# 32x32 block transposes on VectorE for the input and the output of a masked attention, with transfers by quadrants of 32 partitions

## The chip, the cores and the metric

The kernel runs on one core of a Trainium2 chip. Five engines work side by side: TensorE (PE in the profile, its weight loads PEld), VectorE (DVE), ScalarE (ACT), GpSimd (POOL) and SyncE (SP, which here only issues transfers). Each takes its instructions in the order of the program and waits for the others through semaphores. Transfers are issued from the queues of SP, POOL and ACT and are carried by 16 DMA engines. The metric is the time of the whole kernel on the device in microseconds (us), as the median of the runs shown. The three runs before the change took 770.23, 771.29 and 773.01 us.

## The reference

The input `x` holds 8 batches of 512 features by 1024 tokens, in float32. The mask `cond_2048` has a 0 or a 1 for each of the 1024 tokens of a batch.

```python
NH = 8; NEG = -1e+30; B, D, T = x.shape; dk = D // NH        # 8, 512, 1024; dk = 64
xt = jnp.transpose(x, (0, 2, 1))
q = xt @ Wq.T
qh = q.reshape(B, T, NH, dk).transpose(0, 2, 1, 3)            # queries, keys and values are the same
scores = scale * jnp.einsum('bhqd,bhkd->bhqk', qh, qh)
cmask = mask[:, None, None, :]
rmask = mask[:, None, :, None]
logits = (scores * cmask + (1.0 - cmask) * NEG) * rmask
attn = jax.nn.softmax(logits, axis=-1)
ctx = jnp.einsum('bhqk,bhkd->bhqd', attn, qh)
ctx = ctx.transpose(0, 2, 1, 3).reshape(B, T, D)
out = ctx @ Wo.T
return x + jnp.transpose(out, (0, 2, 1))
```

A token whose mask is 1 attends to the tokens whose mask is 1. A token whose mask is 0 has logits of 0 everywhere, so its context is the mean of the projected tokens, the same for all of them. About half of the tokens are kept, so a batch needs some 512 real rows and one row for the mean.

## The kernel before

Only kept tokens are computed, in 576 slots (`NK`), cut into five chunks of 128, 128, 128, 128 and 64 (`NC = 5`, `LAST = 4`). The last slot holds the mean token. The rank of each token among the kept ones is worked out in `early`. If a batch kept too many tokens, another function (`attention_of_all_tokens`) would compute everything; it does not run with these inputs.

A batch goes through these steps. `load_batch` brings `x` in as eight tiles of 128 features by 512 tokens. `turn` transposes 128 tokens: TensorE makes four 128x128 transposes into one PSUM bank (L410), ScalarE copies them out (L415), and GpSimd's queue stores them to `xd`, a buffer in HBM with one row per token (L416). `turn` also has ScalarE add up the features for the mean (L425). `search` finds with VectorE which token belongs in each slot (L451), `gather` fetches those rows of `xd` by an indirect DMA (L463), and `collect` turns them back to features by slots, `xc` (L478), and writes the mean into the last slot.

The heads are worked on in pairs, four pairs to a batch and 32 in all. For a pair, `project` computes queries `qT` (L501). `values` turns them to slots by features, `v` (L520), squares `v` with VectorE (L528), and reduces the squares to the largest length (L530, L537). `bias_of` makes of it the shift for the exponentials (L543 to L548). `scores` multiplies a chunk of keys with all queries (L570) and takes the exponentials on ScalarE into `e` (L574). `add_up` sums them with VectorE, two instructions to a chunk (L591). `attend` multiplies `e` with the values (L607), and ScalarE copies the result to `cT` (L623). `inverses` and `invert` make 1/sum and send it through HBM so that it comes back along the free dimension as `rb` (L663 to L685). `contexts` multiplies `cT` by `rb` on VectorE (L695 to L704).

When all four pairs of a batch are done, `output` multiplies the four `cT` with Wo, chunk by chunk (L720), and GpSimd's queue stores the rows to `od` in HBM. `fetch` gathers for each group of 128 tokens its rows of `od` (L791). `finish` transposes four 128x128 blocks on TensorE (L803), adds the input to them on VectorE (L806), and the sum is stored to the output from SP's queue (L808).

The order of all instructions is written by hand. The main loop of `late` goes over pairs p = (b, pr), and in each over the five chunks c. A step of the loop issues, in this order: the scores of chunk c; `add_up` of chunk c-1; at c = 0 the last `add_up` and `invert` of the pair before; `contexts` of the pair before, at c = 2, 3, 3, 4 for pr = 0, 1, 2, 3; at c = 1 `bias_of` the next pair; the work for the next batch; then a share of a list of tasks (`tasks_of`) that TensorE does between scores; then the stores that are due (`issue_stores`). After chunk 4 comes `attend`.

The tasks are the projection and the values of the pair after next, and by pr: for pr = 0 and 1 the turns of batch b+1 (five and three) and `output` of two chunks of batch b-1 each; for pr = 2 `collect` of batch b+1 and the last chunk of `output`; for pr = 3 the eight `finish` of batch b-1. The first `output` of batch b-1 stands in pr = 0 of batch b and needs the `cT` of all four pairs of b-1, the last of which is made by the `contexts` at c = 2 just before it. `search` of batch b+1 is spread over pr = 0, one chunk of slots a step; `gather` stands at the end of pr = 1. In pr = 1 at c = 2 `load_rest` reads `x` of batch b-1 again for the residual; in pr = 2 at c = 0 batch b+2 is loaded. The last batch ends with code of its own (`end_output`, `fetch_last`, `finish_tokens`).

A ring of four PSUM banks (`bank`) serves everything on TensorE but the scores, which have two tiles of two banks. `e` has a ring of six tiles, so VectorE may be most of a pair behind before it holds up a score.

## Time and profile before

| what | value |
|---|---|
| median of three runs | 771.29 us (770.23 to 773.01) |
| the profiled execution | 769.13 us, of which its span 767.4 us |
| mean granted TensorE clock | 0.985 of full speed |
| busy: PE, DVE, ACT, POOL | 721.3, 496.1, 386.8, 200.7 us |
| moved by the 16 DMA engines | 119.52 MB, mean 156 GB/s |
| DMA share by queue: SP (q1), POOL (q0), ACT (q10) | 24.2%, 21.1%, 0.9% |

Times in the profile are in us from the start of the span, if ns is not written. A row for a group of instructions gives the line, the engine, the operation, output and input with their shapes, the number of instructions, their busy time and the mean of one, and then the time that the engine was idle just before them with what ended it. In the chain of waits each piece is the work that held the end at that time. A table by stretches of time gives the busy time of each engine in a stretch, the clock that TensorE was granted (1.00 is full speed), and the share of time in which the DMA engines were busy. PE's instructions overlap, so the length of a run of them in the chain says more than their busy time.

In the middle of the kernel a batch takes about 88.9 us. In the batch from 291 to 380 us its four pairs take 24.6, 23.6, 20.8 and 20.0 us; TensorE is busy for 24.6, 23.6, 20.04 and 19.87 us of them, VectorE for 20.93, 12.32, 12.55 and 15.53 us.

### The profile page before, as it was taken

The page shows a single profiled execution, that of the slowest core. Times are in us where ns is not written, and L with a number is a line of the kernel's source. Part 1 is how long each engine was busy: PE and PEld are TensorE (multiplying, and loading weights), DVE is VectorE, ACT ScalarE, POOL GpSimd, SP SyncE. Part 2 cuts the span into 40 slices and gives each one's busy share as a digit, 9 for nine tenths or more (in the row PEclk, how much of TensorE's full clock was granted, in tenths as well). Part 3 has the DMA queues.
Part 4 walks back from the last instruction along what each step waited for, and adds up shares of the span by engine and source line. Part 5 has one row for each costly group of instructions (what it writes and reads, how often), then busy time and mean ns, then how long its engine had stood idle before and what let it go on. Part 6 is the DMA issues. An engine that isn't in the chain of part 4 may idle for free.

```text
span 767.4 us, 12722 instructions
## 1 busy us (share of the span) xinstructions
PE 721.3 (94%) x4411; PEld 425.1 (55%) x4411; DVE 496.1 (65%) x1495; ACT 386.8 (50%) x783; POOL 200.7 (26%) x264
## 2 busy tenths in 40 slices
PE   6699999999999999999999999999999999899883
PEld 5565565555655556556655556555655566354342
DVE  6287767556975668556984569656785567547453
ACT  3376566644465546545466545645476544245400
POOL 4723003134112413134031432134031340003221
PEclk9899999999999999999999999999999999999996
DMA  7543402556226843447235653357335342146238
GB/s 266 169 166 117 159 18 101 196 165 228 93 108 205 254 166 108 158 144 262 101 141 182 224 195 115 88 207 251 139 128 172 124 135 88 61 155 170 74 128 268
DMA packets 59098, 119.52 MB, mean 156 GB/s; under 512 B 10144, under 2 KB 18400, under 8 KB 59024
## 3 DMA queue, kind: packets, MB, share of 16 engines
q1 hardware_dynamic: 37792, 61.55, 24.2%
q0 software_dynamic: 17008, 54.97, 21.1%
q10 hardware_dynamic: 4224, 2.10, 0.9%
q8 instruction: 37, 0.61, 0.3%
q14 instruction: 37, 0.30, 0.1%
HBM read 75.40 MB, written 43.18 MB: 155 GB/s over the span
## 4 chain that ended last, share of the span: by engine, by line
PE 79%; ACT 5%; DVE 5%; another core or an unknown queue 3%; DMA 3%; issue 2%; POOL 1%; ACTq 0%; POOLq 0%; DVEq 0%
PE s L570 19%; PE av L607 17%; PE pq L501 15%; PE po L720 13%; PE xc L478 4%; PE xt L410 3%; PE o L803 3%; ACT e L574 3%; PE v L520 2%; PE pa L740 2%; DVE junk L591 1%; DMA rank<-ranks 1%; DMA g<-od,origin 1%; ACT v L523 1%
## 5 line engine op out<-in xcount | busy, mean ns | idle before, releaser
L591 DVE CUSTOM_DVE_ANT_0 junk<-e,valid 128x576 f32<-128x576 f32 x256 | 194.9, 761 | 122.4 <-ACT e L574 117.7
L570 PE MATMUL s<-qT 64*128 64x288 f32 (+1 forms) x1280 | 186.3, 434 | 10.6 <-ACT e L574 9.7
L574 ACT ACTIVATE e<-s,bias 128x576 f32<-128x576 f32 x256 | 176.1, 740 | 34.2 <-PE s L570 23.3
L570 PEld LDWEIGHTS s<-qT 64*128 64x128 f32 (+1 forms) x1280 | 93.7, 175 | 97.1 <-issue 58.5
L501 PE MATMUL pq<-xc,wqT 128*128 128x288 f32 x512 | 138.9, 414 | 0.5 <-issue 0.5
L607 PE MATMUL av<-e,v 128*64 128x288 f32 x1024 | 132.6, 409 | 0.8
L720 PE MATMUL po<-woT,cT 128*128 128x512 f32 (+1 forms) x336 | 117.3, 532 | 2.3 <-DVE cT L703 2.3
L501 PEld LDWEIGHTS pq<-xc,wqT 128*128 128x128 f32 x512 | 92.2, 190 | 34.6 <-issue 8.1
L416 POOL DMA_DIRECT2D xd<-xt x64 | 35.5, 558 | 251.3 <-ACT xt L415 250.9
L607 PEld LDWEIGHTS av<-e,v 128*64 128x64 f32 x1024 | 71.0, 137 | 53.5 <-issue 7.2
L623 ACT COPY cT<-av 128x288 f32<-128x288 f32 x62 | 22.3, 401 | 144.5 <-PE av L607 95.3
L720 PEld LDWEIGHTS po<-woT,cT 128*128 128x128 f32 (+1 forms) x336 | 48.2, 173 | 54.7 <-issue 44.1
L729 POOL DMA_DIRECT2D od<-oc x42 | 23.1, 550 | 199.7 <-ACT oc L727 199.7
L791 POOL DMA_INDIRECT g<-od,origin x56 | 59.6, 1065 | 46.0 <-issue 15.7
L508 ACT COPY qT<-pq 128x288 f32<-128x288 f32 x64 | 25.4, 397 | 67.0 <-PE pq L501 64.6
L528 DVE TENSOR_TENSOR sq<-v 128x640 f32<-128x640 f32 x32 | 26.3, 823 | 43.0 <-ACT v L523 36.7
L727 ACT COPY oc<-po 128x512 f32<-128x512 f32 (+1 forms) x35 | 19.2, 550 | 57.0 <-PE po L720 57.0
L463 POOL DMA_INDIRECT xin<-xd,source x40 | 41.6, 1039 | 18.5 <-issue 9.4
L451 DVE TENSOR_SCALAR_CACHE_REDUCE junk<-rank,key 128x1024 f32<-128x1024 f32 (+4 forms) x40 | 40.1, 1002 | 4.1 <-DMA rank<-ranks 2.7
L806 DVE TENSOR_TENSOR xr<-o,xr 128x512 f32<-128x512 f32 x56 | 36.4, 684 | 5.1 <-PE o L803 2.6
L415 ACT COPY xt<-xt 128x512 f32<-128x512 f32 x64 | 35.4, 591 | 2.4 <-PE xt L410 2.1
L425 ACT ACTIVATE junka<-x 128x512 f32<-128x512 f32 x56 | 35.7, 637 | 1.3
(131 smaller groups left out, 698.6 us busy)
## 6 DMA issues: line engine op xcount, KB each, us to landing
xd<-xt POOLq DMA_DIRECT2D x64, 256.0 KB
xr<-in_x_dram SPq DMA_DIRECT2D x64, 256.0 KB
x<-in_x_dram SPq DMA_DIRECT2D x56, 256.0 KB
out_dram<-xr SPq DMA_DIRECT2D x56, 256.0 KB
rb<-row SPq DMA_DIRECT2D x60, 160.0 KB
od<-oc POOLq DMA_DIRECT2D x28, 256.0 KB
rank<-ranks SPq DMA_DIRECT2D x6, 512.0 KB
x<-in_x_dram POOLq DMA_DIRECT2D x8, 256.0 KB
```

Source lines behind the costliest of these rows:

```text
L416: nc.gpsimd.dma_start(xds[b][i * P : (i + 1) * P, :], xt)
L425: nc.scalar.activation(junk, xs[b][d, r], AF.Copy, accum_out=to)
L451: nc.vector.tensor_scalar(junk[:, :n], rank[:, i * P :], key[:, col], 0.0, ALU.is_le, ALU.add, accum_out=found[:, col])
L463: nc.gpsimd.indirect_dma_start(out=xin[:n, :], out_offset=None, in_=xds[b], in_offset=bass.IndirectOffsetOnAxis(ap=searches[b][2][:n, i : ...
L501: nc.tensor.matmul(pq[:, :KH], wqT[:, d, pr * P : (pr + 1) * P], xcs[b][:, d, cols], start=(d == 0), stop=(d == ND - 1),)
L570: nc.tensor.matmul(s[to, h, :KH], qT[heads[h], keys], qT[heads[h], queries], start=True, stop=True)
L574: nc.scalar.activation(e[:, hf if c < LAST else 0, :, :], s[:, :, :KH], AF.Exp, bias=biases[pair][:, c : c + 1], scale=SCALE,)
L591: nc.vector.tensor_tensor_reduce(junk[:, :n].rearrange("p (f k) -> p f k", k=KH), e[:, :, h, :], (valid if c < LAST else part).rearrange(" ...
L607: nc.tensor.matmul(av[head, :KH], v[keys, c, head], e[keys, hf if c < LAST else 0, h, :], start=(c == 0), stop=(c == LAST),)
L720: nc.tensor.matmul(po[k * n : (k + 1) * n, :w], cTs[b, pr][:, i * P : i * P + n], woT[:, pr, k * w : (k + 1) * w], start=(pr == 0), stop=( ...
L791: nc.gpsimd.indirect_dma_start(out=g, out_offset=None, in_=ods[b], in_offset=bass.IndirectOffsetOnAxis(ap=origin[:, b, i : i + 1], axis=0),)
L806: nc.vector.tensor_tensor(xr, pt, xr, ALU.add)
```

## The change

Five things are changed together.

1. For batches 1 to 7 the input is turned by VectorE. `x` is loaded with four neighbouring features in a partition, as two tiles of 128 x 4 x 512. A `turn` is now one VectorE instruction that transposes 32x32 blocks over 256 tokens (128 x 1024 elements), so there are four turns to a batch in place of eight. The turned tile is stored to `xd` by four transfers, one for each quadrant of 32 partitions, from SP's queue, in runs of 512 bytes. The turns stand at (pr, c) = (0, 0), (0, 2), (0, 4) and (1, 1). Batch 0 is turned on TensorE as before (`turn_first`).
2. ScalarE still adds up the features, now as eight steps of their own over pr = 0 and 1. Because of the new order of features the sums go through HBM and back by two small transfers (`mean_of`).
3. For batches 0 to 5 (`BLOCKS`) the output is turned by VectorE too. `fetch` uses other indices (`block_origin`), so that a 32x32 block transpose of the fetched rows gives features by tokens. `finish_blocks` transposes 128 x 512 elements on VectorE and adds the input on VectorE. The eight of a batch stand at c = 2, 3 and 4 of pr = 3 (two each) and at c = 0 and c = 1 of pr = 0 of the next batch. `load_rest` and the store of the output use four transfers a batch, each of 32 partitions, in runs of 1024 bytes; before there were eight each, of 128 partitions in runs of 2048 bytes.
4. `search` moves from pr = 0 to pr = 1.
5. The squares in `values` are taken by ScalarE.

Batch 6 is still finished on TensorE, at the end, and batch 7 by its own code.

```diff
+    def turn_first(i):
+        r, at = divmod(i * P, NB)
+        pt = bank(f"xt_0_{i}")
+        for d in range(ND):
+            nc.tensor.transpose(pt[:, d * P : (d + 1) * P], xs[0][r][:, d, at : at + P], ident)
...
     def turn(b, i):
-        r, at = divmod(i * P, NB)
-        pt = bank(f"xt_{b}_{i}")
-        for d in range(ND):
-            nc.tensor.transpose(pt[:, d * P : (d + 1) * P], xs[b][d, r][:, at : at + P], ident)
...
-        nc.scalar.copy(xt, pt)
-        nc.gpsimd.dma_start(xds[b][i * P : (i + 1) * P, :], xt)
-        if i % G == G - 1 and b:
-            means(b, r)
+        n = T // NQ
+        r, at = divmod(i * n, NB)
...
+        nc.vector.transpose(
+            xt.rearrange("p k (f d) -> p k d f", d=ND),
+            xs[b][r][:, :, at : at + n].rearrange("p d (k t) -> p k d t", t=Q),
+        )
+        def store():
+            for a in range(A):
+                to = xds[b][i * n : (i + 1) * n, a * P : (a + 1) * P]
+                nc.sync.dma_start(
+                    to.rearrange("(k t) c -> t k c", t=Q), xt[a * Q : (a + 1) * Q, :, :]
+                )
+        stores[1].append(store)
...
+    def mean_of(b):
+        total = sb.tile([P, ND], F32, tag="total", name=f"total_{b}")
+        nc.vector.tensor_tensor(total, xbars[b][:, :, 0], xbars[b][:, :, 1], ALU.add)
...
+        nc.sync.dma_start(row, total)
+            nc.sync.dma_start(xmeans[b], row.rearrange("(a f) d -> (f d) a", a=A))
...
-        nc.vector.tensor_tensor(sq, v, v, ALU.mult)
+        nc.scalar.activation(sq, v, AF.Square)
...
     def load_rest(b):
+        xr = sb.tile([P, D // Q, T // A], F32, tag="xr", name=f"xr_{b}", bufs=1)
+        if b in BLOCKS:
+            for a in range(A):
+                nc.sync.dma_start(xr[a * Q : (a + 1) * Q, :, :], in_blocks(x[b])[a])
...
+    def finish_blocks(b, i):
+        o = sb.tile([P, D // Q, Q], F32, tag="o", name=f"o_{b}_{i}", bufs=2)
+        nc.vector.transpose(o.rearrange("p k t -> p (k t)"), gs[b, i])
+        xr = xrs[b]
+        to = xr[:, :, i * Q : (i + 1) * Q]
+        nc.vector.tensor_tensor(to, o, to, ALU.add)
+        if i == NT - 1:
+            def store():
+                for a in range(A):
+                    nc.sync.dma_start(in_blocks(out[b])[a], xr[a * Q : (a + 1) * Q, :, :])
+            stores[0].append(store)
...
+        TURN = [(0, 0), (0, 2), (0, 4), (1, 1)]
+        FINISH = {
+            (ND - 1, 2): (0, 1),
+            (ND - 1, 3): (2, 3),
+            (ND - 1, 4): (4, 5),
+            (0, 0): (6,),
+            (0, 1): (7,),
+        }
...
                 if b + 1 < B:
-                    if pr == 0:
+                    if (pr, c) in TURN:
+                        turn(b + 1, TURN.index((pr, c)))
+                    if pr < 2 and pr * NC + c < NN * ND:
+                        add_features(b + 1, pr * NC + c)
+                    if pr == 1 and c == LAST:
+                        mean_of(b + 1)
+                    if pr == 1:
                         search(b + 1, c)
...
+                if p == 2 and c == 2:
+                    place_blocks()
+                for i in FINISH.get((pr, c), ()):
+                    of = b - 1 if pr == ND - 1 else b - 2
+                    if of in BLOCKS and of >= 0:
+                        finish_blocks(of, i)
```

## The prediction

> **What bounds the kernel now.** I read the page's totals and its chain first.
>
> ```profile
> PE 721.3 (94%) x4411; PEld 425.1 (55%) x4411; DVE 496.1 (65%) x1495; ACT 386.8 (50%) x783; POOL 200.7 (26%) x264
> PE 79%; ACT 5%; DVE 5%; another core or an unknown queue 3%; DMA 3%; issue 2%; POOL 1%; ACTq 0%; POOLq 0%; DVEq 0%
> PE s L570 19%; PE av L607 17%; PE pq L501 15%; PE po L720 13%; PE xc L478 4%; PE xt L410 3%; PE o L803 3%; ACT e L574 3%; PE v L520 2%; PE pa L740 2%; DVE junk L591 1%; DMA rank<-ranks 1%; DMA g<-od,origin 1%; ACT v L523 1%
> ```
>
> TensorE carries the end, and the transposes that go, xt and o, are on the chain. By that alone the change would pay. VectorE, at 65%, gets the work, but a share of 65% is an average, so I asked for the groups by shape, for the chain through one batch, and for the timeline where pr = 3 meets the next pr = 0.
>
> ```profile
> L410 PE MATMUL xt<-ident,x 128*128 128x128 f32 x256 | 36.0, 287 | 0.0
> L803 PE MATMUL o<-ident,g 128*128 128x128 f32 x224 | 30.9, 278 | 0.0
> L806 DVE TENSOR_TENSOR xr<-o,xr 128x512 f32<-128x512 f32 x56 | 36.4, 684 | 5.1 <-PE o L803 2.6 <-issue 2.5
> L528 DVE TENSOR_TENSOR sq<-v 128x640 f32<-128x640 f32 x32 | 26.3, 823 | 43.0 <-ACT v L523 36.7 <-ACT el L574 3.2 <-issue 3.1
> L677 DVE STREAM_TRANSPOSE rt<-ris 128x32 f32<-128x32 f32 x30 | 6.3, 212 | 1.0
> L950 DVE COPY spread<-totals 64x256 f32<-64x256 f32 x1 | 0.3, 285 | 0.0
> ```
>
> To see: the mean of a TensorE transpose is not its price, since they overlap; the only VectorE transpose here is 32 elements long.
>
> The chain through the batch from 291 to 380 us gives prices:
>
> ```profile
> 299.22 1.17 PE s L570 x8
> 300.39 1.02 PE xt L410 x8
> ...
> 316.91 1.46 PE xt L410 x12
> ...
> 364.79 1.31 PE o L803 x12
> ```
>
> And the place that decides, in the timelines of an ordinary batch and of batch 7:
>
> ```profile
> 363.61 0.76 DVE L591 CUSTOM_DVE_ANT_0 junk<-e,valid 128x576 f32<-128x576 f32 x1 [3.57 <-ACT e L574]
> 389.76 3.70 PE L720 MATMUL po<-woT,cT 128*128 128x512 f32 x8
> 390.65 0.76 DVE L703 TENSOR_TENSOR cT<-cT,rb 128x576 f32<-128x576 f32 x1
> ```
>
> ```profile
> 653.08 2.84 PE L720 MATMUL po<-woT,cT 128*128 128x512 f32 x6
> 657.44 0.76 DVE L703 TENSOR_TENSOR cT<-cT,rb 128x576 f32<-128x576 f32 x1
> 658.26 1.41 PE L720 MATMUL po<-woT,cT 128*128 128x512 f32 x2 [2.33 <-DVE cT L703]
> ```
>
> `output` needs the fourth `cT` for its last two matmuls of eight. In the ordinary batch they are due at 389.8 + 6 x 0.456 = 392.5 (the chain has 3.65 us for eight) and `cT` is ready at 391.4: about 1 us of slack, and VectorE has worked almost without a pause since 363.61. Batch 7 has no turns behind it; there TensorE came early and stood for 2.33 us. So in pr = 3 and the start of the next pr = 0 VectorE is already nearly the bound.
>
> ```profile
> 656.00:658.00 2.00, 0.00 (x0) 0.00 (x0) 1.86 (x7) 0.00 (x0) 0.00 (x0) 1.00 0.00 0
> 658.00:660.00 2.00, 1.74 (x4) 0.71 (x6) 1.79 (x6) 0.30 (x1) 0.00 (x0) 0.74 0.00 0
> 660.00:662.00 2.00, 2.00 (x9) 0.96 (x8) 0.00 (x0) 1.09 (x3) 0.59 (x1) 0.50 0.14 59
> 662.00:664.00 2.00, 2.00 (x5) 0.98 (x6) 1.26 (x3) 0.67 (x1) 0.00 (x0) 0.90 0.19 76
> ```
>
> After that wait the granted clock (third column from the end) fell to 0.50. From 658.26 to the next `attend` at 666.42 took 8.16 us; the same pieces in an ordinary batch take 0.9 + 1.17 + 3.63 + 0.65 = 6.35. The clock cost 1.8 us.
>
> **The change part by part.**
>
> *Off TensorE.* A batch loses 4.1 us in pr = 3 (pieces of 12, 4, 8, 4 and 4 transposes: 1.31 + 0.59 + 1.02 + 0.59 + 0.59), 2.3 in pr = 0 (0.87 + 0.44 + 1.02) and 1.46 in pr = 1. Over 6 finished and 7 turned batches that is 6 x 4.1 + 7 x 3.8 = 51 us. This is the most that can be won.
>
> *Price of a VectorE transpose.* No row shows a long one. Low end: L950, 285 ns for 256 elements against 153 ns for a one-element copy (L704), 0.52 ns an element, so 0.42 us for 512 and 0.69 for 1024. High end: L677, 212 ns for 32 against 153 for one, 1.9 ns an element, so 1.13 and 2.1. I take one element a cycle, as every two-input row (0.68 for 512, 0.82 for 640): 0.71 and 1.24, because L677 stands only 20 ns above what those rows give for 32. Back to back each hides some 0.08 us of its tail behind the next, unless that one needs its result.
>
> *VectorE from the first `add_up` of pr = 3 (363.61) to `cT` in the next pr = 0 (391.41): 27.8 us.* Off: eight adds, 8 x 0.62 = 5.0; one square, 0.85; `search` 0 and 1, 1.40 + 1.24; short waits for TensorE and `rb` that a later VectorE no longer has, 1.3. On: eight `finish_blocks`, transpose 0.74 with its gap, then add 0.62, 10.9; turn 0, 1.16; length and top of the values, 0.93, which stood behind `contexts` and now stand ahead (TensorE reaches `values` at c = 1). Sum: +3.2 us, so `cT` at 394.6. TensorE is there 6.4 us earlier, at 386.1, and waits 8.5 us. It resumes 394.6 - 392.5 = 2.1 us later than before, and loses 1.8 us by the clock: **+3.9 us**, five times (batches 1 to 5 into the next) = +19.5. Into batch 7 there is no turn, and the wait and the lost clock were there before: 628.03 + 29.2 = 657.2 against 658.2, -0.9.
>
> *pr = 1.* Six times -1.46 = -8.8. VectorE takes five searches (5.9) and turn 3, less a square: 12.3 + 5.9 + 1.2 - 0.8 = 18.6 of 22 us. The last `source` comes about 2 us before the pair's end, while the fifth gather was issued 1.3 us after it until now. If that cover is gone `collect` is late: +1 to 2 a batch.
>
> *Batch 0.* The chain stands on ranks for 7.6 us until 42.1 and then on VectorE to 60. With searches gone from pr = 0 TensorE needs 17.8 of the 21.6 us: -3.8. The next pair loses 1.46 and gets five searches (VectorE 18.8, TensorE 14.9); I give back 1.8. Sum -3.5. In batch 1's pr = 0, 2.3 us of turns go, and a wait of some 1.6 us and perhaps the clock come: 0, between -2.3 and +1.
>
> *Early part.* Eight sums of 512 (5.4 us, on the chain) become two of 2048, by the slope 2.3 each: -0.9. `place_blocks`, 16 copies of some 0.15 in batch 0's third pair, where VectorE is idle 8 us of 21: nothing; uncovered 2.4.
>
> *ScalarE.* 56 copies of 0.59 go (33), 32 squares of some 0.75 come (L425's 0.64 for 512), 24. The squares stand before the copies of `cT`, under `attend`'s 4.7 us, or beside scores: nothing; each could delay an exponential by 0.75.
>
> *Queues.* POOL loses 56 issues of 0.55 that nobody waited for. SP gains 112 stores of some 0.35 and 14 transfers of the mean, and loses 48. It waits for a turn, but its next urgent item, the rows of `invert`, comes only in the next pair; behind turn 3 stands only `load_rest`. The mean's two hops, like `invert` to `rb`, take about 8 us, and there are some 11 till `project` needs them. The 512-byte runs to HBM cost nothing extra: ACT's queue moved 4224 packets of about 500 bytes for 0.9% of the 16 engines, 26 ns each, no dearer by the byte than SP's 79 ns for 1629. Quadrants: no row shows a long transfer of 32 partitions. From nothing up to `rb` 3 us late; I take nothing, since the turned rows are issued behind `rb`.
>
> *Sum:* 19.5 - 0.9 - 8.8 - 3.5 - 0.9 = **+5.4 us**. The profiled execution took 769.1 us, span 767.4, so 774.5 there; the median was 771.3, 2.2 above it, so **776.7**.
>
> The Trainium skill, "TensorE: Matmul & The Clock Gate", "Why this matters for your kernels", asks for no idle gaps over about 3 us. The trace is harsher, as 2.33 us sufficed. By the page's window of 3.4 us at half speed a wait would cost 1.7 us in place of 1.8, and the sum would be 0.5 lower. "SBUF — State Buffer", "Door 1: The DMA port swizzle", speaks against the change: 32 partitions reach 8 of 16 ports, 189 GB/s. By it a reload of 2 MB is an estimated 11 us, against about 5.5 at the 380 to 400 GB/s seen here with 128; the sum gets no term, because pr = 1 has room for it.
>
> **The rivals.**
>
> *The relief comes whole* (faster): 771.3 - 51 = 720. For it: the chain's 79%. Against: `cT` would have to come 8.5 us earlier.
>
> *Cheap transposes* (faster): at the low end the stretch is 8 x 0.29 + 0.55 = 2.9 shorter, 5 x 2.9 + 2.3 = 17 less: 760. For it: L950. Against: L677.
>
> *The clock holds*: 5 x 1.8 less, 768. For it: at 712 to 716 TensorE was idle for 2.2 us and the clock stayed 1.00. Against: at 16 to 24 and at 746 to 750 longer gaps halved it.
>
> *Dear transposes* (slower): at the high end 8 x 0.42 + 0.86 = 4.2 longer, 5 x 4.2 + 3.4 = 24 more: 801.
>
> *Transfers late* (slower): `rb` came 7.8 us after its transpose, and four of five such `contexts` waited 0.27 to 0.69 us for it. It has some 0.5 us to spare now. With 3 us of delay, five times 2.5: 789.
>
> **How the numbers follow.** About 0.3% (2.3 us) can be told from no change. Forecast 0.45 (own range 768 to 786), cheap transposes 0.12, clock holds 0.10, whole relief 0.04, dear transposes 0.15, late transfers 0.14. Slower: 0.32 + 0.15 + 0.13 = 0.60. Same: 0.07 of the forecast and 0.06 of the clock and the transfers. Faster: the remaining 0.27. Range 757 to 801, from the two ends of the transpose.
>
> **What would show it.** A 512-element STREAM_TRANSPOSE near 0.71 us; "PE po <- DVE cT L703" near 8 us in each of six batches, with clock 0.50 after it; VectorE without idle time from pr = 3 to that `cT`; pr = 1 about 1.4 us shorter. I am wrong if TensorE does not wait there, if `collect` or `rb` waits for a DMA, or if exponentials come late behind squares.

## The result and the profile after

The change made the kernel slower: 817.8 us (median, 814.8 to 823.5) against 770.8 for the kernel before beside it, a ratio of 1.0625 (95% interval 1.0551 to 1.0699). I had forecast 776.7. The direction was right and the size was not. The profiled execution took 823.5 us, with a span of 821.7.

First the totals and the chain of the kernel after, by engine and by line.

```profile
PE 707.9 (86%) x3995; PEld 393.8 (48%) x3995; DVE 556.7 (68%) x1550; ACT 381.7 (46%) x759; POOL 165.6 (20%) x208
...
PE 52%; DVE 25%; DMA 9%; issue 7%; ACT 4%; POOL 1%; SPq 0%; another core or an unknown queue 0%; POOLq 0%; DVEq 0%; ACTq 0%
PE s L614 12%; PE po L764 12%; PE av L651 11%; PE pq L545 9%; DMA xin<-xd,source 6%; DVE junk L635 6%; DVE o L841 3%; DVE xr L844 3%; ACT e L618 3%; DVE xt L446 2%; PE xc L524 2%; DVE junk L497 2%; DVE cT L747 2%; PE pa L784 1%; DVE len L574 1%
```

TensorE's share of the chain fell from 79% to 52%. VectorE took 25% in place of 5%. And there is a newcomer that my sum didn't hold: the gather of tokens, `xin`, with 6%. TensorE's busy time fell by only 13 us although 416 instructions are gone, because much of the rest ran at a lower clock (mean 0.927 in place of 0.985).

The groups by shape give the prices that were unknown:

```profile
L446 DVE STREAM_TRANSPOSE xt<-x 128x1024 f32<-128x1024 f32 x28 | 57.6, 2059 | 0.4 <-DMA rank<-ranks 0.4
L841 DVE STREAM_TRANSPOSE o<-g 128x512 f32<-128x512 f32 x48 | 33.8, 704 | 0.0
L844 DVE TENSOR_TENSOR xr<-o,xr 128x512 f32<-128x512 f32 x48 | 33.2, 693 | 1.6
L574 DVE TENSOR_REDUCE len<-sq 128x10 f32<-128x640 f32 x32 | 26.0, 813 | 33.3 <-ACT sq L572 22.6 <-issue 8.4 <-ACT v L567 2.3
```

The transpose of 512 elements took 0.70 us, as forecast. The one of 1024 took 2.06, where I had put 1.24. The last line shows something I had costed at nothing: VectorE stood 22.6 us for ScalarE's squares.

The waits (in total, times, longest) and the places where they stand in TensorE's timeline (the number in brackets is the idle time before the instruction):

```profile
PE po L764 <- DVE cT L747: 48.3, 7, 8.4
PE xc L524 <- DMA xin<-xd,source: 31.1, 8, 9.4
```

```profile
362.89 1.09 PE L524 MATMUL xc<-ident,xin 128*128 128x128 f32 x4 [4.29 <-DMA xin<-xd,source]
...
408.09 2.84 PE L764 MATMUL po<-woT,cT 128*128 128x512 f32 x6
418.87 2.08 PE L764 MATMUL po<-woT,cT 128*128 128x512 f32 x2 [7.94 <-DVE cT L747]
```

The stall for the fourth `cT` is the one I forecast: 7.8 to 8.4 us in batches 2 to 6, 5.3 in batch 7, 2.8 in batch 1. VectorE worked without a pause between these two rows, from the first `add_up` of pr = 3 to that `cT`:

```profile
387.23 0.76 DVE L635 CUSTOM_DVE_ANT_0 junk<-e,valid 128x576 f32<-128x576 f32 x1 [3.54 <-ACT e L618]
...
418.06 0.76 DVE L747 TENSOR_TENSOR cT<-cT,rb 128x576 f32<-128x576 f32 x1
```

The stall for `xin` is the one I missed: at the start of pr = 2, `collect` waits 3.4 to 4.3 us for the gathered tokens, in six batches. (The 31.1 us also hold the 9.4 us at the kernel's start, which were there before.)

To see what each costs I took the starts of `attend` from TensorE's timeline. The table has the time from the `attend` of the pair before to that of the pair named, medians over batches 2 to 6, worked out from those starts.

| us | pr = 0 | pr = 1 | pr = 2 | pr = 3 | batch |
|---|---|---|---|---|---|
| before | 24.5 | 23.6 | 20.7 | 20.1 | 88.9 |
| after | 33.4 | 22.6 | 26.1 | 16.0 | 98.1 |
| forecast | +8.0 | -1.5 | 0 | -4.1 | +2.4 |
| measured | +8.9 | -1.0 | +5.4 | -4.1 | +9.2 |

The forecast for pr = 3 and pr = 0 together was +3.9, of which -4.1 lay in pr = 3; +4.8 was measured. So one column is far off, pr = 2: 5.4 us a batch where the sum had none. What it waits for is in the timelines of SP and POOL and in the windows (busy time of PE, PEld, DVE, ACT and POOL, granted clock, share of the DMA engines, GB/s) of the same batch:

```profile
345.83 1.86 SPq L454 DMA_DIRECT2D xd<-xt  x4
347.73 2.14 SPq L829 DMA_DIRECT2D xr<-in_x_dram  x4
...
353.43 1.03 POOL L509 DMA_INDIRECT xin<-xd,source  x1 [0.56 <-DVE cT L748]
```

```profile
348.00:350.00 2.00, 2.00 (x6) 0.80 (x6) 1.93 (x6) 0.72 (x2) 0.00 (x0) 1.00 0.88 215
350.00:352.00 2.00, 2.00 (x13) 0.56 (x11) 1.86 (x8) 0.55 (x1) 0.00 (x0) 1.00 0.99 221
...
354.00:356.00 2.00, 2.00 (x20) 1.20 (x18) 1.93 (x9) 0.28 (x1) 1.51 (x2) 1.00 1.12 205
356.00:358.00 2.00, 2.00 (x22) 0.93 (x20) 1.93 (x7) 0.31 (x1) 1.58 (x2) 1.00 1.12 189
358.00:360.00 2.00, 0.61 (x6) 0.15 (x2) 1.62 (x11) 0.49 (x2) 1.27 (x2) 1.00 1.10 223
360.00:362.00 2.00, 0.00 (x0) 0.00 (x0) 0.00 (x1) 1.37 (x2) 0.00 (x0) 0.64 1.05 390
362.00:364.00 2.00, 1.10 (x6) 0.81 (x8) 1.53 (x4) 0.00 (x0) 0.00 (x0) 0.50 0.75 263
```

SP issues in order. The reload of x stands behind the four stores of turn 3, turn 3 comes late from a full VectorE, and so the reload starts at 347.7, 13.0 us after pr = 1's first scores (334.8). In the kernel before it started 2.8 us after them (at 318.5; the scores at 315.7). The DMA engines then look full (share 0.88 to 0.99 before the gather, 1.05 to 1.12 with it) and move only 189 to 223 GB/s until 360. The gather is issued at 353.4 into the middle of that. In the kernel before the reload ran in windows like these, and the first gather was issued at 335.1, when it was long over:

```profile
318.47 5.79 SPq L771 DMA_DIRECT2D xr<-in_x_dram  x8
335.12 1.04 POOL L463 DMA_INDIRECT xin<-xd,source  x1 [0.38 <-issue]
...
322.00:324.00 2.00, 2.00 (x6) 0.95 (x5) 0.69 (x4) 1.73 (x5) 0.00 (x0) 1.00 1.02 380
324.00:326.00 2.00, 2.00 (x11) 0.88 (x9) 1.30 (x4) 0.68 (x2) 0.00 (x0) 1.00 1.01 390
```

### The profile page after: what moved, and what is told of

Same layout as the page of the kernel before. It is cut to its first block, busy times and chain, and to the rows that moved or that the text cites. A ratio compares the mean times of both kernels' runs of the same rounds, so it can differ in the third digit from the quotient of the medians.

```text
span 821.7 us, 11761 instructions
## 1 busy us (share of the span) xinstructions
PE 707.9 (86%) x3995; PEld 393.8 (48%) x3995; DVE 556.7 (68%) x1550; ACT 381.7 (46%) x759; POOL 165.6 (20%) x208
## 4 chain that ended last, share of the span: by engine, by line
PE 52%; DVE 25%; DMA 9%; issue 7%; ACT 4%; POOL 1%; SPq 0%; another core or an unknown queue 0%; POOLq 0%; DVEq 0%; ACTq 0%
PE s L614 12%; PE po L764 12%; PE av L651 11%; PE pq L545 9%; DMA xin<-xd,source 6%; DVE junk L635 6%; DVE o L841 3%; DVE xr L844 3%; ACT e L618 3%; DVE xt L446 2%; PE xc L524 2%; DVE junk L497 2%; DVE cT L747 2%; PE pa L784 1%; DVE len L574 1%
## 5 line engine op out<-in xcount | busy, mean ns | idle before, releaser
L614 PE MATMUL s<-qT 64*128 64x288 f32 (+1 forms) x1280 | 193.7, 447 | 6.7 <-ACT e L618 4.7
L764 PE MATMUL po<-woT,cT 128*128 128x512 f32 (+1 forms) x336 | 139.3, 637 | 48.3 <-DVE cT L747 48.3
L614 PEld LDWEIGHTS s<-qT 64*128 64x128 f32 (+1 forms) x1280 | 96.9, 182 | 103.5 <-issue 61.9
L764 PEld LDWEIGHTS po<-woT,cT 128*128 128x128 f32 (+1 forms) x336 | 54.9, 208 | 113.7 <-issue 58.0
L446 DVE STREAM_TRANSPOSE xt<-x 128x1024 f32<-128x1024 f32 x28 | 57.6, 2059 | 0.4 <-DMA rank<-ranks 0.4
L870 POOL DMA_INDIRECT g<-od,block_origin x48 | 50.2, 1046 | 34.6 <-issue 30.3
L589 DVE TENSOR_REDUCE m<-top 128x1 f32<-128x128 f32 x32 | 9.3, 290 | 68.8 <-PE top L587 68.8
L524 PE MATMUL xc<-ident,xin 128*128 128x128 f32 (+1 forms) x160 | 24.5, 296 | 34.5 <-DMA xin<-xd,source 31.1
L574 DVE TENSOR_REDUCE len<-sq 128x10 f32<-128x640 f32 x32 | 26.0, 813 | 33.3 <-ACT sq L572 22.6
L635 DVE CUSTOM_DVE_ANT_0 junk<-el,part 128x288 f32<-128x288 f32 x64 | 29.1, 454 | 15.2 <-ACT el L618 13.9
```

The source lines that it names most:

```text
L446: nc.vector.transpose(xt.rearrange("p k (f d) -> p k d f", d=ND), xs[b][r][:, :, at : at + n].rearrange("p d (k t) -> p k d t", t=Q),)
L524: nc.tensor.transpose(pt[:, d * n : (d + 1) * n], xin[:n, d * P : (d + 1) * P], ident[:n, :n])
L574: nc.vector.tensor_reduce(lengths, sq.rearrange("p c (h d) -> p (c h) d", h=2), axis=AX.X, op=ALU.add,)
L614: nc.tensor.matmul(s[to, h, :KH], qT[heads[h], keys], qT[heads[h], queries], start=True, stop=True)
L635: nc.vector.tensor_tensor_reduce(junk[:, :n].rearrange("p (f k) -> p f k", k=KH), e[:, :, h, :], (valid if c < LAST else part).rearrange(" ...
L764: nc.tensor.matmul(po[k * n : (k + 1) * n, :w], cTs[b, pr][:, i * P : i * P + n], woT[:, pr, k * w : (k + 1) * w], start=(pr == 0), stop=( ...
```

## The experiments

The kernel before did not take the same time in all comparisons: about 759 us in some, 770 to 776 in others (the last experiment looks at this). Ratios are always to the kernel before beside it. Times are compared directly only where the kernel before took 758.7 to 759.2 us beside both; there the changed kernel took 815.1 us, ratio 1.0733 (1.0705 to 1.0762).

> The changed kernel itself, so that the other three runs stand beside it on one chip: ratio 1.055 to 1.07.

It came out a little above, since the kernel before was faster there. The stalls were the same: 7.8 to 8.0 us for `cT` in batches 2 to 6, 3.5 to 4.3 for `xin`.

### The reload: its place and its width

Place alone:

```diff
-                if pr == 1 and c == 2 and b > 0:
+                if pr == 1 and c == 0 and b > 0:
                     load_rest(b - 1)
```

> The changed kernel with one edit: load_rest(b - 1) is called at (pr 1, c 0) in place of (pr 1, c 2), so that its four transfers stand ahead of turn 3's stores on SP's queue. In the profile after, TensorE stands 3.4 to 4.3 us at the first xc of pr = 2 in six batches (sum 23.1 us), and the clock is granted at 0.50 to 0.66 for some 6 us after it. Theory 'queue place': SP waits for turn 3, issues the reload 12.9 us after the pair's start, and the gather shares the DMA engines with it. Then here the reload is issued within 4 us of the pair's start, is over before the gather at about +18.6 us, the wait for xin is under 1 us each, and the time falls by 23 to 35 us, to about 786. Rival 'the gather is late by itself' (the last source comes from a full VectorE at +18.4 us): the waits stay at 3 to 4 us and the time stays within 4 us of 818.

Width and length of runs:

```diff
-            for a in range(A):
-                nc.sync.dma_start(xr[a * Q : (a + 1) * Q, :, :], in_blocks(x[b])[a])
+            wide = xr.rearrange("p k n -> p (k n)")
+            for i in range(NN * ND):
+                r, d = divmod(i, ND)
+                nc.sync.dma_start(
+                    wide[:, i * NB : (i + 1) * NB],
+                    x[b, d * P : (d + 1) * P, r * NB : (r + 1) * NB],
+                )
```

> The changed kernel with the reload at its late place, but as eight transfers of 128 partitions with runs of 2 KB, as the kernel before had it, in place of four of 32 partitions with runs of 1 KB. The features of x then stand at other places of xr than the rows that are added to them, so that the output isn't the reference's; the work and the bytes are the same. Theory 'rate': the reload ran at 190 to 220 GB/s from 348 to 360 us in the profile after, while the kernel before moved the same bytes at 380 to 400. Here it takes 5 to 6 us from +12.9, ends at about +18.5 as the gather begins, the wait for xin falls below 1.5 us each and the time falls by 15 to 35 us. If only the place on the queue matters, part of the overlap stays and the waits stay above 2 us; if the gather is late by itself, nothing changes.

Width alone, with runs of 1 KB in four transfers as in the change:

```diff
-            for a in range(A):
-                nc.sync.dma_start(xr[a * Q : (a + 1) * Q, :, :], in_blocks(x[b])[a])
+            wide = xr.rearrange("p (j k) n -> j p k n", j=A)
+            parts = x[b].rearrange("(k p) (j n) -> j p k n", p=P, j=A)
+            for j in range(A):
+                nc.sync.dma_start(wide[j], parts[j])
```

> The changed kernel with the reload at its late place, in four transfers of 512 KB with runs of 1 KB, as in the change, but each over 128 partitions in place of 32. The features of x then stand at other places of xr than the rows added to them, so that the output isn't the reference's; bytes, runs and places on the queue are the same. Theory 'partitions': the reload takes 5 to 7 us in place of some 12 and the waits for xin fall below 2.5 us, as in the kernel with wide transfers and runs of 2 KB (784 us where the changed kernel took 815). Rival 'length of the runs': it takes 10 us or more, the waits stay at 3.4 to 4.3 us, and the time stays within 6 us of the changed kernel's.

| | us | ratio | pr = 2 |
|---|---|---|---|
| the change | 815.1 | 1.0733 (1.0705 to 1.0762) | 25.9 |
| reload ahead of turn 3 | 786.7 | 1.0354 (1.0323 to 1.0385) | 20.2 |
| reload in 128 partitions, 2 KB | 784.2 | 1.0342 (1.0324 to 1.0360) | 20.5 |
| reload in 128 partitions, 1 KB | 782.0 | 1.0292 (1.0260 to 1.0325) | 20.2 |

Each of the three brings pr = 2 back to its old length, so it takes both causes to make the stall: a reload that is late and one that is slow. Each is worth 28 to 33 us. This is the largest part of the loss that I missed. In the first of the three the reload was issued 2.2 us after pr = 1's first scores. The last run separates what the second had changed together: the same bytes in the same runs of 1 KB, but over 128 partitions, moved in these windows:

```profile
340.00:342.00 2.00, 2.00 (x15) 0.73 (x13) 1.86 (x7) 1.08 (x2) 0.29 (x1) 1.00 1.08 355
342.00:344.00 2.00, 2.00 (x18) 1.20 (x18) 1.93 (x6) 1.63 (x4) 1.28 (x2) 1.00 1.10 360
344.00:346.00 2.00, 2.00 (x18) 1.00 (x14) 1.93 (x8) 0.00 (x0) 1.55 (x2) 1.00 1.07 382
```

355 to 382 GB/s against 189 to 223 at the same share of the engines: the partitions make the difference, not the runs. The fast windows end at 346, some 9 us after the reload was issued (337.1) behind turn 3's stores, so the 5 to 7 us are not shown; the waits for `xin` behind the start of the kernel came to 2.8 us in all. The Trainium skill, "SBUF — State Buffer", "Door 1: The DMA port swizzle", gives 189 GB/s for 32 partitions at 1 MiB and about 218 as the limit; the two windows before the gather, 215 and 221, agree. The prediction had an estimate of 11 us from that page, and I then gave it no term.

The wait for `cT` did not move with any of this, here in the run with the reload ahead:

```profile
PE po L764 <- DVE cT L747: 47.6, 7, 8.1
PE xc L524 <- DMA xin<-xd,source: 15.5, 7, 9.7
```

### The price of the turn

```diff
         nc.vector.transpose(
-            xt.rearrange("p k (f d) -> p k d f", d=ND),
+            xt.rearrange("p k (d f) -> p k d f", d=ND),
```

> The changed kernel with the turn's output written block behind block (32 elements in a row) in place of with a stride of 4 elements. The features of a row of xd then stand in another order, so that the output isn't the reference's; count and size of all instructions and transfers are the same. Theory 'stride of the output': the instruction of 1024 elements falls from 2.06 to between 1.25 and 1.40 us (twice the 0.70 us of the 512-element one, which is written densely). It stands once on VectorE's chain to cT (0.7 us, five or six times, 4 us) and once on that to the gather (0.7 us, six times, 4 us): 6 to 9 us less in all. Rival 'stride of the blocks that are read' (a new row of d every 32 elements) or 'two ports, other cause': it stays at 2.06 us and the time stays the same.

```profile
L446 DVE STREAM_TRANSPOSE xt<-x 128x1024 f32<-128x1024 f32 x28 | 34.8, 1241 | 0.4 <-issue 0.4
```

Written densely, 1024 elements took 1.241 us, which is the price I had taken. The stride of four elements in what it writes makes it 2.06. The waits for `cT` fell from 7.8 to 7.1 us, and the time was 803.1 us, ratio 1.0584 (1.0542 to 1.0625), 12 us below the changed kernel: a little more than the 6 to 9 expected. By the starts of `attend`, pr = 0 became 5.8 us shorter in all and pr = 2 4.7, so that part of these 12 us lies within the stall for `xin`.

### One part of the change alone

The input part, with outputs turned on TensorE as before:

```diff
-    BLOCKS = range(B - 2)
+    BLOCKS = range(0)
...
+            elif b + 1 < B:
+                t = 0.5
+                back += [(t, lambda r=r, d=d: finish(b - 1, r, d)) for r in range(NN) for d in range(ND)]
```

> The changed kernel with BLOCKS = range(0) and the eight finish tasks of 0.5 back in pr = 3: tokens turned on VectorE, outputs turned on TensorE as before, reload in 128 partitions. Theory 'two stalls make the loss' (the wait for cT at 7.8 to 8.4 us in five batches from finishes and turn 0 on VectorE; the wait for xin from the quadrant reload): here VectorE loses 8 x 0.64 us ahead of cT, so the wait for cT is 0 to 3 us, the wait for xin 0 to 1.5 us, and what TensorE loses in transposes (7 x 3.8 us) is a gain in part: 750 to 768, centre 757. Rival 'turn 0 and the searches in pr = 1 are what cost, whatever becomes of the output': 775 or above, waits for cT above 4 us or for xin above 3 us.

766.0 us, ratio 1.0100 (1.0082 to 1.0118): inside the band in us, but the gain that the text counted on did not come, since the kernel before took 758.7 beside it. The wait for `cT` is 2.8 us in six batches and 2.2 in the seventh (18.9 in all) and the clock is at 0.50 for some 3.4 us after it, which eats what TensorE no longer does.

The output part alone, in the kernel before (`finish_blocks`, its reload, its places as in the change):

> The kernel before with the output part alone: eight finish_blocks of VectorE for each of batches 0 to 5 in place of TensorE's transposes, with the reload by quadrants at its old place (to fit the memory, xt has 4 buffers and pa lies in those of xin). Theory of the two stalls: VectorE gets 8 x (0.64 + 0.69) less 8 x 0.62 and some waits, 4.4 us, ahead of the fourth cT; TensorE comes 4.1 us earlier against 1 us of slack: it waits 7 to 7.5 us in five or six batches, resumes 3.3 us later than in the kernel before and loses some 1.8 us of clock, so +5 us each: ratio 1.03 to 1.045. The reload starts 3 us into pr = 1 with no turns ahead of it, so no wait for xin over 1 us. Rival 'the output part is harmless by itself and only meets turn 0 badly': ratio 0.97 to 1.00, waits for cT under 4 us.

Ratio 1.0264 (1.0186 to 1.0341), a little below the expected band, though its interval reaches into it, and not in the form expected. TensorE's waits in that run:

```profile
PE po L722 <- DVE cT L705: 17.8, 6, 7.0
PE s L572 <- ACT e L576: 15.6, 32, 1.5
PE v L522 <- DVE m L547: 9.6, 5, 1.9
...
PE top L545 <- DVE top L539: 6.6, 6, 1.2
```

The wait came in pieces: 1.2 us for `top`, 1.9 for `m` and 1.5 to 3.2 for `cT` in each of the five batches, 6.95 only in the last. All three are results of VectorE, in pr = 0, which took 31.1 us in place of 24.5.

The squares alone:

```diff
-        nc.vector.tensor_tensor(sq, v, v, ALU.mult)
+        nc.scalar.activation(sq, v, AF.Square)
```

> The kernel before with the squares alone moved: sq by ScalarE's Square in place of VectorE's product. My prediction put this part at nothing. Theory 'hidden': ratio to the kernel before 0.995 to 1.003. Rival 'a new wait': in the input-only kernel VectorE stood 1.95 us for ScalarE's square directly ahead of add_up and contexts (len L574 <- ACT sq), and in the profile after 22.6 us in six such waits; if that happens here too, up to eight times 2 to 4 us, and where it delays cT, 1.005 to 1.03.

Ratio 0.9991 (0.9952 to 1.0029): nothing, as predicted. The three parts add up to 0.0100 + 0.0264 - 0.0009 = 0.0355, and the change with its reload ahead has 0.0354. That they agree so well proves little: the kernel before took 776.2 us beside the last two parts and 758.7 beside the others. What the waits do show is that the stall for `xin` comes only when the parts meet. With the input part alone these waits make 6.0 us in all behind the start of the kernel, with the output part alone there are none. The late turn 3 of the one pushes the slow reload of the other into the gather.

### Is it the order of the work, or a full VectorE?

The stall for `cT` has two sides: VectorE is late, and TensorE asks early. First I let TensorE ask later, with the outputs of the batch before a whole pair later:

```diff
-                mine = {0: (0, 1), 1: (2, 3), 2: (4,)}[pr]
+                mine = {0: (), 1: (0, 1, 2), 2: (3, 4)}[pr]
```

> The whole change with the reload ahead of turn 3's stores (ratio 1.0354), and the output tasks moved a pair later as in the run beside it. There TensorE waited 7.8 to 8.1 us for the fourth cT in five batches, 2.8 and 5.3 in two others (47.6 us), with about 3.5 to 6 us of half clock after each. Theory 'order, not load': VectorE's late cT is needed 7.2 us of work later, the five waits fall below 1.5 us each, 45 to 60 us less, ratio 0.955 to 0.98: the change then pays. Rival 'VectorE is the bound in pr = 3 to pr = 0': add_up and contexts stay late, the wait comes back at bias, at the exponentials or at the first output of pr = 1, ratio 1.00 to 1.035.

> The input-only kernel (ratio 1.0100) with one edit: the output tasks of batch b - 1 stand at pr = 1 (0, 1, 2) and pr = 2 (3, 4) of batch b in place of pr = 0 (0, 1), 1 (2, 3) and 2 (4), so that 7.2 us of TensorE's work that needs the fourth cT stands a pair later. In the input-only run TensorE waited 2.8 us for that cT in six batches and 2.2 in the seventh (18.9 us) with the clock at 0.50 for some 3.5 us after it (1.7 us each). Theory 'TensorE's work was put in an order that needs cT too early': these waits go, 25 to 31 us less, ratio 0.96 to 0.98, and the transposes taken off TensorE (27 us) come through. Rival 'VectorE or ScalarE bounds pr = 0 anyway': other waits of the same sum take their place (for e, for rb, for project's copies), ratio 0.99 to 1.01.

With the whole change the rival was right, and more than that: ratio 1.0607 (1.0536 to 1.0678), worse than 1.0354 (in us 825.1 against 786.7). The wait for `cT` is gone, and pr = 0 takes 16.1 us in place of 32.7. But pr = 1 now takes 26.9 and pr = 2 35.7. The chain of that run shows where the time went:

```profile
332.47 2.07 DVE xt L446
...
338.46 1.21 SPq L454
339.71 1.26 SPq L454
341.01 10.58 DMA xd<-xt
...
352.38 3.31 DMA xin<-xd,source
355.82 1.09 PE xc L524 x4
```

VectorE worked from 288 to 338 with hardly a pause (9.4 to 9.7 us of each 10). TensorE ran ahead of it through the pair, and what came late then was turn 3; its stores needed 10.6 us beside the reload, and TensorE waited 9.3 to 10.0 us for `xin` in five batches. A stall that is moved without its cause comes back where the next result of the full engine is needed.

With the input part alone, ratio 0.9935 (0.9901 to 0.9970). The waits for `cT` went, and waits for `e` of 3.0 to 4.5 us appeared at pr = 3 in five batches. There ScalarE itself stood for something that the trace doesn't name (2.48 us at 453.7), as it did in the kernel before (the last experiment). That is what the rival had said, in number and in kind. Spreading the same input part further (turns at (0, 2), (0, 3), (0, 4), (1, 0), and one output a pair later) brought nothing measurable:

> The input-only kernel (ratio 1.0100, waits for cT of 2.8 us) with turn 0 behind the contexts of pr = 0, turns at (0, 2), (0, 3), (0, 4), (1, 0), and one output a pair later. Theory 'place': the waits for cT go (18.9 us and some 12 us of clock) and those for xin too; ratio 0.965 to 0.985. With no output in pr = 0 at all (ratio 0.9935) waits for e of 3 to 4.5 us took their place at pr = 3; if these are there here too, 0.985 to 0.995.

Ratio 0.9992 (0.9953 to 1.0030), with the same waits for `e`, above both bands that I had given. Both runs stood beside a kernel before of 772 to 776 us and had stalls of that unnamed kind themselves, so what the order of the input part is worth without them stays open.

Then I took the work away from the place where VectorE is full: the finishes run a batch later, where VectorE has room.

```diff
         FINISH = {
-            (ND - 1, 2): (0, 1),
-            (ND - 1, 3): (2, 3),
-            (ND - 1, 4): (4, 5),
-            (0, 0): (6,),
-            (0, 1): (7,),
+            (2, 0): (0,), (2, 1): (1,), (2, 2): (2,), (2, 3): (3,), (2, 4): (4,),
+            (3, 0): (5,), (3, 1): (6,), (3, 2): (7,),
         }
...
-                if pr == 1 and c == 2 and b > 0:
-                    load_rest(b - 1)
-                if pr == 3 and c == 0 and b > 0:
+                if pr == 1 and c == 0 and b > 1:
+                    load_rest(b - 2)
+                if pr == 3 and c == LAST and b == B - 1:
+                    load_rest(b - 1)
+                if pr == 3 and c == 3 and b > 0:
                     fetch(b - 1)
...
-                    of = b - 1 if pr == ND - 1 else b - 2
+                    of = b - 2
```

> The whole change with its eight finish_blocks a batch later: five in pr = 2 (one a step) and three at the start of pr = 3, the gather of the outputs at (pr 3, c 3), the reload at (pr 1, c 0) of that batch, ahead of turn 3's stores. Nothing is left out; VectorE does the same work. With the finishes at their first place and the reload ahead, the ratio was 1.0354 and TensorE waited 7.8 to 8.1 us for the fourth cT in five batches. Theory 'place on VectorE': 10.7 us leave the stretch from pr = 3's first add_up to that cT, the wait falls to the 2.8 us of the input-only kernel, and what TensorE no longer turns (51 us) comes through in part: ratio 0.955 to 0.985. Rival 'VectorE is too full anywhere' (with the outputs a pair later, the 7.9 us came back as a wait for xin of 9 to 10 us): pr = 2 now has the late add_up, waits for e or cT of pr = 1 of the same sum appear there, ratio 1.01 to 1.04.

Ratio 0.9801 (0.9734 to 0.9868) where the kernel before took 772.2 us. Where it took 759.1, the same kernel gave 756.8 us and 0.9967 (0.9945 to 0.9990), outside what I had expected, because the kernel before was faster there; the waits came as said:

> The kernel with the finishes a batch later, once more: ratio 0.973 to 0.987, waits for the fourth cT of 2.2 to 3.1 us in seven batches.

```profile
PE po L764 <- DVE cT L747: 19.0, 7, 2.8
```

VectorE does as much work as in the change, and the time is 58 us less than the changed kernel's 815.1. Against the run with only the reload ahead (786.7) it is 30 us, and pr = 0 shows them: 26.8 us in place of 32.7. (In the profiles pr = 0 is 38 us shorter in all seven batches together, and the end of the kernel is 8 us longer, where TensorE now waits up to 7.4 us for gathered outputs.) So place is what cost, not the amount of work. A wait of 2.8 us for `cT` stayed. The prediction's own step would put it on turn 0, so I moved turn 0 behind it, first together with one output, then alone:

```diff
-        TURN = [(0, 0), (0, 2), (0, 4), (1, 1)]
+        TURN = [(0, 2), (0, 3), (0, 4), (1, 0)]
```

> As the run beside it, and with turn 0 behind the contexts of pr = 0 (turns at (0, 2), (0, 3), (0, 4), (1, 0)) and one output of batch b - 1 a pair later (1, 2 and 2 in pr = 0, 1 and 2). Theory 'place': turn 0's 2.1 us leave the way to cT too, and the output that needs it comes 3.6 us later: waits for cT under 1 us, turn 3 earlier by some 6 us, no wait for xin, ratio 0.945 to 0.965. Rival 'VectorE too full': no better than the run beside it, or above 1.00.

> The finishes a batch later, and the turns alone at (0, 2), (0, 3), (0, 4), (1, 0), so that turn 0 comes behind the fourth cT. By the prediction's step (turn 0 stands on the way to cT: 1.16 us, 2.06 as measured) it gains 7 x 2 = 14 us at most, ratio 0.96 to 0.975. Rival: the turns are bunched, VectorE and SP fall behind in pr = 1 and the gather comes late, as in the run with the output moved too (waits for xin of 3.2 to 6.5 us, ratio 1.0112): 1.00 to 1.015.

Neither gained. The first was slower, 1.0112 (1.0047 to 1.0177): pr = 0 shrank to 21.8 us, but pr = 2 grew to 29.9, with waits for `xin` of 3.2 to 6.5. With the turns alone pr = 2 is 20.4, so that was the moved output. The turns alone: 763.1 us, 1.0050 (1.0028 to 1.0073), 6 us slower than beside it, and the wait for `cT` still 2.8 to 3.1 in six batches. The rows of ScalarE, VectorE and TensorE there show what it hangs on:

```profile
381.22 0.75 ACT L568 COPY v<-v 128x512 f32<-128x512 f32 x2
...
382.00 0.74 ACT L573 ACTIVATE sq<-v 128x640 f32<-128x640 f32 x1
...
382.77 0.82 DVE L575 TENSOR_REDUCE len<-sq 128x10 f32<-128x640 f32 x1 [1.95 <-ACT sq L573]
...
386.51 0.76 DVE L748 TENSOR_TENSOR cT<-cT,rb 128x576 f32<-128x576 f32 x1
...
387.32 2.08 PE L765 MATMUL po<-woT,cT 128*128 128x512 f32 x2 [2.80 <-DVE cT L748]
```

VectorE is not full here. It stands 1.95 us for ScalarE's square, because the length of the values is ahead of `contexts` in its order, and the values themselves have just come from TensorE; from there to `cT` it works without a pause. With no transposes to do in pr = 0, TensorE reaches `values` and then the outputs sooner than this round can close. That is read from one batch's rows: no run gave the squares back to VectorE in this kernel. So at last I let TensorE ask one step later, not a whole pair:

```diff
                 mine = {0: (0, 1), 1: (2, 3), 2: (4,)}[pr]
+                if pr == 0:
+                    end.append((6.0, lambda: None))
```

> The kernel with the finishes a batch later (ratio 0.9801), and in pr = 0 an empty task of weight 6.0 ahead of the two outputs of batch b - 1, so that they come at c = 3 and 4 in place of 2 and 3, behind one more step of scores. There TensorE still waited 2.8 to 3.1 us for the fourth cT in six batches and 2.2 in the seventh (19.2 us), and lost about 1.7 us of clock after each: rb is issued at 381 to 382 us, cT is ready at 388.1, TensorE runs out of work at 385.3. Theory 'TensorE asks too early': the waits go, some 25 to 31 us less, ratio 0.94 to 0.955. Rival 'the round trip only shows elsewhere' (e late, oc copied late at the start of pr = 1, as with the outputs a whole pair later): ratio 0.97 to 0.985, with waits of 2 to 4 us at another place.

> The same with the outputs of pr = 0 one step later, where the profile showed no wait for cT but one of 1.67 us for e. If such a stall costs its length and the clock after it (2.8 + 1.7 us, less 1.7 for the new one), it is 6 x 2.8 = 17 us below the run beside it, a ratio lower by 0.02. Rival: what the stall held up was not on the path for long, and the ratio is within 0.005 of the run beside it.

Ratios 0.9833 (0.9765 to 0.9902) and 0.9846 (0.9822 to 0.9870), both where the kernel before took 759 us. The first lies in its rival's band, not in its theory's. This kernel beats both: 747.6 us against 759.1 and 815.1 beside one another. The wait is now 1.67 us, for `e`, and the clock stayed at 1.00 after it:

```profile
372.60 1.39 PE L614 MATMUL s<-qT 64*128 64x288 f32 x8 [1.67 <-ACT e L618]
373.92 3.71 PE L764 MATMUL po<-woT,cT 128*128 128x512 f32 x8
```

It is 9.2 us faster than the run beside it, where I had expected 17; pr = 0 is 2.8 us shorter in the ordinary batch (24.0 for 26.8), but in two batches only 1.2, since there the old wait had cost no clock (25.2), and in some batches pr = 2 gave part of it back (21.1 and 23.6 in place of 19.9). The rival, under 0.005, is out as well: the difference is 0.012.

### The kernel before, twice

> The kernel before, for its profile on another chip. It took 769.1 us in the profile shown first. If this chip is one of those where it takes about 759 us, theory 'waits': some of the stalls of ScalarE and TensorE that end with no known releaser at the start of pr = 3 (27 us of ScalarE's time in four places) are missing or shorter; rival 'clock': the granted clock is higher in the same stages.

It took 759.4 us, ratio 0.9997 (0.9983 to 1.0010) to the kernel before beside it. In the profile shown first ScalarE stood like this, at the start of pr = 3 ("remote" is a releaser that the profile doesn't name):

```profile
ACT cT L623 <- remote: 27.0, 4, 7.1
```

In the second profile there is no such wait, and the chain has no "another core or an unknown queue", which had 3% in the first. The clock is no higher (mean 0.980 against 0.985). pr = 2 and pr = 3 take 19.9 and 19.0 us in place of 20.7 and 20.1, which is 1.9 us a batch. So theory "waits" holds. What ScalarE waits for neither trace shows, and why it is there in some comparisons only stays open. For the study it means that some 10 us of the kernel before can hide in a comparison, and that a ratio's interval holds for its own comparison. It is not the chip alone: on chip 1 the kernel before took 772.2 us beside one set of runs and 759.2 beside a later one. Against the kernel before without these stalls the change costs more than the first ratio says, 1.0733.

## Why the prediction was wrong

By its own steps:

- *Off TensorE, pr = 3*: -4.1 forecast, -4.1 measured, but that is partly luck: the 20.1 us of the kernel before hold its unnamed stalls, and against the 19.0 without them the gain is 3.0. *pr = 1*: -1.5 forecast, -1.0 measured, and the last source was no problem by itself: with the reload out of the way the waits for `xin` were at most 2.2 us.
- *VectorE from the first `add_up` of pr = 3 to `cT`*: 31.0 us forecast, 31.6 measured (387.23 to 418.82), a wait of 8.5 forecast, 7.8 to 8.4 measured. The mechanism was right, down to the batches in which it stands. Into batch 7, -0.9 was forecast and +1.3 measured.
- *Price of a transpose*: right for 512 (0.70), wrong for the turn. I priced it by its elements and overlooked that it writes with a stride. The sum held 1.24, it measured 2.06, close to the 2.1 of the high end that I had named myself. Taken back alone this gave 12 us, some 5 of them in pr = 2.
- *The clock*: I took 1.8 us from batch 7. After a wait of 2.8 us the clock stayed at 0.50 for some 3.4 us, which agrees. After the five of 7.8 to 8.4 us TensorE worked 3.9 to 6.5 us at half clock (418.9 to 425.3 in the batch shown), so that 2.0 to 3.2 us were lost.
- *ScalarE*: "nothing" holds for the squares alone. But the length and top of the values, which I had rightly seen move ahead of `contexts`, brought a wait for the square with it, which by the rows shown stands on the way to the 2.8 us that remained once the finishes were elsewhere; that it is the limit is not tested.
- *Batch 0 and the early part*: -4.4 forecast. The first `attend` came 2.1 us earlier, and the rest of batch 0 gained nothing: the `attend` of its second pair came 2.4 us sooner after the first, the next one 2.5 later. The first pair of batch 1, put at nothing, took 2.3 us more.
- *The step that failed*: "behind turn 3 stands only `load_rest`", and of the reload at half the rate "the sum gets no term, because pr = 1 has room for it". I had both halves in hand. `load_rest` behind turn 3 is not harmless when turn 3 is the last thing a full VectorE does in that pair: the reload began 10 us later within the pair than before. And the room in pr = 1 is measured from that start to the gather, 5.7 us (347.7 to 353.4), not over the whole pair; a reload of some 12 us doesn't fit in it. My "cover" for the late `collect`, +1 to 2 us, was priced by when the gather is issued, not by what the DMA engines are doing then, and it did not enter the sum. Measured: 5.4 us a batch; taking either half away gave 28 to 33 us.

The two profiled executions show what each term took, by the starts of `attend` (batches 1 to 6, and pr = 3 with the next pr = 0):

| us | forecast | measured |
|---|---|---|
| start, batch 0 and pr = 0 of batch 1 | -4.4 | +0.2 |
| pr = 3 into the next pr = 0 | +18.6 | +24.2 |
| pr = 1 | -8.8 | -5.7 |
| pr = 2 | 0 | +33.7 |
| the rest | 0 | +1.8 |
| sum | +5.4 | +54.3 |

So pr = 2 is two thirds of the miss of 48.9 us. The other third is spread over small terms, and the dearer turn has a share in both. (This execution was the slowest of the four; by the medians the change cost 47 us.) The rival "transfers late" was near, but it named `rb`; `rb` never became a wait of TensorE. The signs that I had listed came nearly as said (0.70 us, some 8 us in five batches, VectorE without idle time, pr = 1 shorter by 1.0), and one of those that were to prove me wrong, "`collect` or `rb` waits for a DMA", came too.

## What to carry to other kernels

When an engine takes over work, ask for each of its results who stands behind it in another queue: a store that waits for a late result holds back every later transfer on that queue, and a transfer that "has room" has it only between its own start and the next user of the DMA engines. Price a moved transfer as start, rate and end against what runs then, not as bytes against a pair. And an engine with a share of 68% can still be the bound for a third of a batch: the same work of VectorE, with its finishes, the reload and two outputs in other places, turned a loss of 7% into a gain of 1.5%.

## What was not expected of the hardware

- A 32x32 transpose on VectorE takes 0.70 us for 512 and 1.24 us for 1024 elements of 32 bits when it writes densely, and 2.06 us for 1024 when the elements it writes are 16 bytes apart.
- The time that TensorE spends at clock 0.50 around a wait comes in steps. In windows of 0.5 us it makes 3.4 us for waits of 2.2 to 2.8 us, where the clock falls at all, and 6.8 or 10.2 us for waits of 7.8 to 8.4: after two waits of the same 7.84 us in the changed kernel, 10.2 at 321 and 6.8 at 517. Part of it falls into the wait itself. The Trainium skill, "TensorE: Matmul & The Clock Gate", "What's actually happening", gives a free-running window of 3413 ns; one, two and three of them are what stands here. Whether a short wait costs anything varies too. In the kernel with the finishes a batch later, the first of two waits of 2.79 us cost no clock and the second did, and pr = 0 took 25.2 and 26.9 us:

```profile
125.29 1.12 PE L764 MATMUL po<-woT,cT 128*128 128x512 f32 x2 [2.79 <-DVE cT L747]
208.97 1.82 PE L764 MATMUL po<-woT,cT 128*128 128x512 f32 x2 [2.79 <-DVE cT L747]
...
126.00:128.00 2.00, 2.00 (x10) 0.98 (x10) 1.97 (x3) 1.44 (x3) 0.65 (x1) 1.00 0.00 0
210.00:212.00 2.00, 2.00 (x7) 1.00 (x8) 1.97 (x4) 0.58 (x1) 0.29 (x1) 0.50 0.04 11
```

- While the reload by 32 partitions ran, all 16 DMA engines looked full (share 0.99 before the gather, 1.05 to 1.12 with it) and moved 189 to 223 GB/s; with the same runs over 128 partitions they moved 355 to 382 at a share of 1.07 to 1.10. So the share alone does not show the loss.
